# The head of a two-layer attention kernel: idle products, the place of the first projection, centred weights, maxima as a step

## The chip, the cores and the metric

The kernel runs on one core of a Trainium2 chip. The metric is the device time of one execution in microseconds (us), as the median of several runs. In the profile PE is TensorE, PEld its weight loads, DVE is VectorE, ACT is ScalarE, POOL is GpSimd, and SP is the engine that issues most DMAs.

## What is computed

Input x has 8 images of 128 channels and 48 x 48 positions (N = 2304). Layer 0 is a masked attention over positions, on the group-normed input joined to 32 rows of position embeddings. Layer 1 is a full attention of the tokens with themselves, then a normalized linear layer with a recurrence over tokens.

```python
# layer 0
x0 = concat([_gn(x), pe], axis=1)                # _gn: 32 groups of 4 channels
q = lrelu(Wq @ x0 + bq); k = lrelu(Wk @ x0 + bk); v = lrelu(Wv @ x0 + bv)
attn = q.T @ k / sqrt(128), masked to the lower triangle
x = x + softmax(attn) @ v
# layer 1
t = tokens(x)
t = t + softmax(n @ n.T) @ n                     # n = _ln_t(t)
Wx = _ln_t(t) @ W.T, normalized over all images and tokens
y[i] = sigmoid(Wx[i] + y[i-1] @ V.T)             # over the tokens, y[-1] = 0
t = t + y
```

## The kernel before

One image after another goes through `Causal` (layer 0) and `Full` (attention of layer 1); the recurrence over all images comes last. N is cut into six chunks of 384 columns (`NQ = 6`, `QC = 384`), and each chunk into three blocks of 128 (`QB = 3`). For each pair of a key block m and a query chunk j there is a score product s (one bank of the four of pool `ps_s`), an exponential on ACT into p, and three items later (`LAG = 3`) an output product o. In float32 a product of 384 columns is two instructions. In the masked part VectorE also adds up p into `acc`.

Ahead of its scores a chunk n needs its projection, `project(b, n)`: `normed` applies the group norm (L872), and three `part`s each make a product with the weights of q, k or v (L879, L882; also in banks of `ps_s`), add the chunk's position term `pb` (L884) and apply the leaky ReLU (L889). In the third part follow two reductions that give the largest |q| and |k| (L893), the load of the position term of chunk n + 2 (`load_positions`, L850), and the next projection. Two projections' xn can exist at a time, and four q.

The position terms are the same for every image. `positions(n, j)` makes them from 33 rows (32 embeddings and the bias, L837 and L840), ACT copies them out (L841), and they are stored in DRAM once per chunk (L843, on SP's queue). Those of chunks 0 and 1 also stay on chip for the first image; all others are loaded again, into two buffers. The steps for chunks 2 to 5 form a chain named `making`; loading chunk n first advances it to 3 (n - 1) steps.

The order of instructions on every engine is written out by hand. A planner, `Stream`, holds a modelled time `now` and the time at which each engine is free. Work that isn't part of the main stream of scores and outputs is a chain of steps, each with a cost on TensorE, further costs on other engines, and a due time. After every item of the stream, `tick` runs up to two steps that are due, in the order in which the chains were added. `advance` and `finish` run a chain's steps regardless of the due time. These planned times only fix the order in which instructions are issued; the engines wait for each other through semaphores.

At the start of the program x is loaded in three pieces on SP (L711), followed there by half of the position rows, w, V and gamma and beta (L741 to L744). TensorE runs 12 idle products of the identity with itself (L1383), then the position products of chunk 0. The group norm of image 0 is three parts: BN_STATS and BN_AGGR on VectorE (L796, L798), a product with `grp` that averages over a group (`gn_m`, L804), three small VectorE operations to `gn_e`, a second product (`gn_v`, L815), and a power on GpSimd (L665). Position products of chunk 1 lie between these. Then `project(0, 0)` is added, and the stream starts; its first item finishes that projection. `ffn_weights` (L746 to L756), due at a planned 30 us, centres w on VectorE, transposes it on TensorE, and makes V times one half; both products go into one bank.

The later projections are started in three places: chunks 1 and 2 at the end of the projection before them (`if n + 1 < EARLY`, with `EARLY = 3`), chunks 3 to 5 by row j = 0 to 2 of the stream (`begin`), and chunk 0 of the next image near the end of `Full`.

Of the kernel before, what the change touches and what calls it, by code (L numbers as in the profile page):

```python
# [16 lines left out]
ALU = mybir.AluOpType  # L17
AX = mybir.AxisListType
# [586 lines left out]
def fast_path(ctx: ExitStack, tc: tile.TileContext, x, pe, w_ffn, out, x_tok, w_qkv, w_pos, v_t, gamma_beta, flag):  # L605
# [61 lines left out]
    with ExitStack() as actx:  # L667
# [19 lines left out]
        def psum_t(name):  # L687
            return ps_t.tile([P, CH], F32, tag="t", name=name)
# [16 lines left out]

        xbuf = {}

        def load_x(b, pieces=2):
            xbuf[b] = big.tile([P, N], F32, tag="x", name=f"x_{b}")
            for h in range(pieces):  # L710
                nc.sync.dma_start(xbuf[b][:, ts(h, N // pieces)], x_v[b, :, ts(h, N // pieces)])  # L711

        load_x(0, 3)


        cg = C // GROUPS
# [26 lines left out]
        nc.sync.dma_start(vT_f, v_t)  # L743
        nc.sync.dma_start(gb, gamma_beta)  # L744

        def ffn_weights():  # L746

            s = small.tile([P, 1], F32, tag="gn_d", name="w_sum")
            nc.vector.tensor_reduce(s, w1, AX.X, ALU.add)
            nc.vector.tensor_scalar_mul(s, s, 1.0 / P)  # L750
            nc.vector.tensor_scalar(w1, w1, s, None, ALU.subtract)
            tp = psum_t("tp_ffn")
            nc.tensor.transpose(tp[:, 0:P], w1, ident)
            nc.vector.tensor_copy(w1T, tp[:, 0:P])
            nc.tensor.matmul(tp[:, P : P + 1], vT_f, half, start=True, stop=True)
            nc.vector.tensor_copy(v_half, tp[:, P : P + 1])  # L756


        same = apool.tile([P, R, SQ], F32, tag="same", name="same")
# [29 lines left out]
        def group_norm(b):  # L789
            xt = xbuf[b]  # L790
            c = {}

            def part1():
                gs = small2.tile([P, NQ, 6], F32, tag="gn_st", name=f"gn_st_{b}")
                for j in range(NQ):
                    nc.vector.bn_stats(gs[:, j, :], xt[:, ts(j, QC)])  # L796
                mv = small2.tile([P, 2], F32, tag="gn_mv", name=f"gn_mv_{b}")
                nc.vector.bn_aggr(mv, gs)  # L798
                c["mv"] = mv

            def part2():
                mv = c["mv"]
                tp = psum_t(f"gn_m_{b}")
                nc.tensor.matmul(tp[:, 0:1], grp, mv[:, 0:1], start=True, stop=True)  # L804
                mg = small2.tile([P, 1], F32, tag="gn_mg", name=f"gn_mg_{b}")
                nc.vector.tensor_copy(mg, tp[:, 0:1])
                d = small.tile([P, 1], F32, tag="gn_d", name=f"gn_d_{b}")
                nc.vector.tensor_sub(d, mv[:, 0:1], mg)
                e = small2.tile([P, 1], F32, tag="gn_e", name=f"gn_e_{b}")
                nc.vector.scalar_tensor_tensor(e, d, d, mv[:, 1:2], ALU.mult, ALU.add)  # L810
                c["mg"], c["e"] = mg, e

            def part3():
                tp = psum_t(f"gn_v_{b}")
                nc.tensor.matmul(tp[:, 0:1], grp, c["e"], start=True, stop=True)  # L815
                rs = small2.tile([P, 1], F32, tag="gn_rs", name=f"gn_rs_{b}")
                rsqrt(small2, rs, tp[:, 0:1], 1e-5, "gn")
                norm_of[b] = c["mg"], rs

            return [(part1, 0.0, [("DVE", 3.6)]), (part2, 0.15, [("DVE", 0.6)]), (part3, 0.15, [("DVE", 0.15), ("POOL", 0.9)])]  # L820
# [34 lines left out]
        def project(b, n):  # L855

            cols = ts(n, QC)
            c = {}

            def normed():  # L860
                if n > 1:
                    st.finish(projected[b, n - 2])
                if (b, n) in pos_loads:
                    st.finish(pos_loads[b, n])
                c["pb"] = pos.pop((b, n))
                if n == 0:
                    keys[b] = big.tile([P, N], F32, tag="k", name=f"k_{b}")
                    vals[b] = big.tile([P, N], F32, tag="vT", name=f"vT_{b}")
                    largest[b] = small2.tile([P, 2, NQ], F32, tag="largest", name=f"largest_{b}")
                mg, rs = norm_of[b]  # L870
                c["xn"] = chunk_tile("xn", f"xn_{b}_{n}", c, 4)
                nc.vector.tensor_scalar(c["xn"], xbuf[b][:, cols], mg, rs, ALU.subtract, ALU.mult)  # L872

            def part(j):
                def f():
                    xn = c["xn"]
                    ps = psum_s(f"pj_{b}_{n}_{j}")
                    if j < 2:
                        nc.tensor.matmul(ps[:, :QC], wT[:, j, :], xn, start=True, stop=True)  # L879
                    else:  # L880
                        for m in range(0, QC, P):
                            nc.tensor.matmul(ps[:, ds(m, P)], xn[:, ds(m, P)], wT[:, j, :], start=True, stop=True)  # L882
                    z = chunk_tile("z", f"z_{b}_{n}_{j}")
                    nc.vector.tensor_add(z, ps[:, :QC], c["pb"][:, j, :])  # L884
                    if j == 0:
                        queries[b, n] = qp.tile([P, QC], F32, tag="q", name=f"q_{b}_{n}")
                    dst = (queries[b, n], keys[b][:, cols], vals[b][:, cols])[j]

                    nc.vector.scalar_tensor_tensor(dst, z, 0.01, z, ALU.mult, ALU.max)  # L889
                    c[j] = dst  # L890
                    if j == 2:
                        for i in range(2):
                            nc.vector.tensor_reduce(  # L893
                                largest[b][:, i, n : n + 1], c[i], AX.X, ALU.max, apply_absolute_value=True
                            )
                        load_positions(*divmod(b * NQ + n + 2, NQ))
                        if n + 1 < EARLY:
                            project(b, n + 1)
                        if n == NQ - 1 and b + 1 < B:
                            st.add([(partial(load_x, b + 1), 0.0, [])], 5.0)  # L900

                return f

            steps = [(normed, 0.0, [("DVE", 0.75)])]

            steps += [(part(j), QC * US, [("DVE", 0.0 if j < 2 else 4.5)]) for j in range(3)]
            c["chain"] = projected[b, n] = st.add(steps)

        def bounds(b):
# [79 lines left out]
        class Causal:  # L989
# [18 lines left out]
            def begin(self, j, m, first):  # L1008
                b = self.b
                if first:  # L1010
                    st.finish(projected[b, j])
                    if j + EARLY < NQ:
                        project(b, j + EARLY)
                    if j == NQ - 1:
                        bounds(b)
                off = self.offset(j, m)
                s = psum_s(f"s_{b}_{j}_{m}")
                nc.tensor.matmul(s[:, off:QC], keys[b][:, ts(m, P)], queries[b, j][:, off:], start=True, stop=True)  # L1018
                p = pp.tile([P, QC], F32, tag="p", name=f"p_{b}_{j}_{m}")
                nc.scalar.activation(p[:, off:], s[:, off:QC], AF.Exp, scale=SCALE)  # L1020
                ops = [("ACT", 0.16 + (QC - off) * 0.00085)]
                if m >= QB * j:
                    nc.gpsimd.tensor_mul(p[:, off : off + P], p[:, off : off + P], triu)  # L1023
                    ops.append(("POOL", 0.5))
                return p, st.then(st.spend((QC - off) * US), ops)
# [350 lines left out]
                ], max(at, st.free["DVE"]) + 0.2 - st.now)  # L1376

        norm_chain = {}
        st.add([(ffn_weights, 0.3, [("DVE", 0.5)])], 30.0)
        def idle(tp, n):  # L1380

            for _ in range(n):
                nc.tensor.matmul(tp[:, :P], ident, ident, start=True, stop=True)  # L1383

        idle(psum_s("idle"), 12)
        for j in range(3):
            positions(0, j)
        gn = st.add(group_norm(0))
        st.advance(gn, 2)
        positions(1, 0)  # L1390
        st.finish(gn)
        for j in range(1, 3):
            positions(1, j)
        project(0, 0)
        making = st.add([(partial(positions, n, j), QC * US, [("ACT", 0.5)]) for n in range(2, NQ) for j in range(3)], 6.0)


# [13 lines left out]
        for n in range(len(stream) + LAG):  # L1411
            if n < len(stream):
                part, j, what, first, last = stream[n]
                ready[n] = part.begin(j, what, first)
            if n >= LAG:
                part, j, what, first, last = stream[n - LAG]
                if first:
                    o[part, j] = psum_o(f"o_{n}")
                part.product(j, what, o[part, j], *ready.pop(n - LAG), first, last)
                if last:  # L1420
                    part.after(j, o.pop((part, j)))
            st.tick()
# [194 lines left out]
```

## Time and profile before

| | us |
|---|---|
| median of three runs | 1761.54 (1758.81 to 1763.01) |
| profiled execution | 1763.07 |
| its span, first to last instruction | 1761.4 |
| PE busy in the span | 1733.7 |
| scores of `Full`, L1217: 1008 instructions | 409.3 |
| outputs of `Full`, L1231 and L1227: 1728 instructions | 683.8 |
| scores and outputs of `Causal`, L1018 and L1029: 2016 instructions | 761.2 |
| projections, L879: 192 instructions | 80.6 |
| wait of PE for w on VectorE, L753 | 1.5 |
| wait of PE for xn, L879 | 1.4 |
| wait of PE for the aggregated statistics, L804 | 1.4 |
| wait of VectorE for a position load, L884 | 4.4 |

The first four rows frame the run: the profiled execution lies 1.7 us above its own span. The product rows are busy times of TensorE; an instruction there overlaps the next one, so they add up to more than the span. The four waits are all in the first 36 us. "Granted clock" in the views below is the share of its full clock that TensorE was given.

### The profile page before, as it was taken

Reading aid. Unit: us, or ns where it says so; the run is one execution under the profiler, and the core shown is the slowest. Engines: PE = TensorE matmul, PEld = TensorE weight load, DVE = VectorE, ACT = ScalarE, POOL = GpSimd, SP = SyncE. Lnnn points to the kernel's source line nnn. Section 1 sums busy time; section 2 is a strip of 40 time slices with the busy share of each in tenths; the row PEclk is TensorE's granted clock in tenths of the full one; section 3 lists DMA queues with packets and bytes.
Section 4 is the critical chain, followed back from the end, with each engine's and each line's share of the span. In section 5 each row is a group of like instructions: output and inputs, shape, how many; then the busy total and the mean of one; then the engine's idle time right before and its main releaser. Section 6 shows DMA issues by size and latency. Waiting matters only on the chain.

```text
span 1761.4 us, 21442 instructions
## 1 busy us (share of the span) xinstructions
PE 1733.7 (98%) x6134; PEld 1082.0 (61%) x6135; DVE 1159.5 (66%) x3163; ACT 718.9 (41%) x1332; POOL 321.0 (18%) x397
## 2 busy tenths in 40 slices
PE   8999999999999999999999999999999999999986
PEld 5666666656666566666666566665666666665565
DVE  4875569655886459755696557864587556974357
ACT  2344334443344424443244433444344432444345
POOL 1131002300132001410024001320014100240006
PEclk7999999999999999999999999999999999999998
DMA  3415673157533684156731575335941568216768
GB/s 128 144 32 185 174 202 117 63 178 208 161 93 110 182 223 138 41 178 178 205 117 61 181 203 158 99 111 175 229 140 41 172 178 211 62 56 181 204 214 217
DMA packets 206050, 261.94 MB, mean 149 GB/s; under 512 B 90113, under 2 KB 175010, under 8 KB 205412
## 3 DMA queue, kind: packets, MB, share of 16 engines
q1 hardware_dynamic: 204972, 257.47, 50.3%
q0 software_dynamic: 720, 2.62, 1.0%
q8 instruction: 51, 0.84, 0.2%
q14 instruction: 75, 0.61, 0.1%
q10 hardware_dynamic: 232, 0.40, 0.1%
HBM read 150.24 MB, written 110.17 MB: 148 GB/s over the span
## 4 chain that ended last, share of the span: by engine, by line
PE 96%; DMA 1%; DVE 1%; SPq 1%; issue 0%; ACT 0%; POOL 0%; DVEq 0%; ACTq 0%; POOLq 0%
PE s L1217 18%; PE o L1231 18%; PE s L1018 17%; PE o L1029 17%; PE o L1227 13%; PE pj L879 4%; PE pj L882 2%; PE z L1530 2%; PE wx L1306 2%; PE tb L939 1%; PE of_t L939 1%; PE pb L837 0%; DMA x<-in_x_dram 0%; PE dn L1077 0%; DMA t2x<-t_d 0%; DMA out_dram<-r 0%
## 5 line engine op out<-in xcount | busy, mean ns | idle before, releaser
L1219 ACT ACTIVATE p<-s,shift 128x384 f32<-128x384 f32 x504 | 292.5, 580 | 519.0 <-PE s L1217 497.8
L1217 PE MATMUL s<-xh 128*128 128x384 f32 x1008 | 409.3, 488 | 0.0
L1020 ACT ACTIVATE p<-s 128x384 f32<-128x384 f32 (+2 forms) x504 | 231.0, 460 | 427.3 <-PE s L1018 349.3
L1231 PE MATMUL o<-p,xhT 128*128 128x384 f32 x1008 | 402.4, 486 | 1.1 <-ACT p L1219 1.1
L1018 PE MATMUL s<-q,k 128*128 128x384 f32 (+2 forms) x1008 | 382.9, 462 | 0.2 <-DVE k L889 0.2
L1029 PE MATMUL o<-p,vT 128*128 128x384 f32 (+2 forms) x1008 | 378.3, 457 | 0.0
L1227 PE MATMUL o<-g,xhT 128*128 128x384 f32 x720 | 281.4, 486 | 1.1 <-DMA g<-e 1.1
L1188 DVE STREAM_TRANSPOSE t<-p 128x384 f32<-128x384 f32 x360 | 186.1, 550 | 136.2 <-ACT p L1219 97.6
L1231 PEld LDWEIGHTS o<-p,xhT 128*128 128x128 f32 x1008 | 190.2, 190 | 129.2 <-ACT p L1219 1.7
L1217 PEld LDWEIGHTS s<-xh 128*128 128x128 f32 x1008 | 187.4, 190 | 119.5
L1029 PEld LDWEIGHTS o<-p,vT 128*128 128x128 f32 x1008 | 188.5, 191 | 116.1 <-POOL p L1023 3.0
L1018 PEld LDWEIGHTS s<-q,k 128*128 128x128 f32 x1008 | 182.3, 191 | 96.7 <-issue 1.3
L1044 DVE TENSOR_TENSOR acc<-acc,p 128x384 f32<-128x384 f32 (+2 forms) x408 | 213.4, 523 | 26.5 <-POOL p L1023 2.9
L1227 PEld LDWEIGHTS o<-g,xhT 128*128 128x128 f32 x720 | 134.1, 190 | 87.7 <-issue 1.8
L1023 POOL TENSOR_TENSOR p<-p,triu 128x128 f32<-128x128 f32 x144 | 77.8, 544 | 528.9 <-ACT p L1020 527.6
L884 DVE TENSOR_TENSOR z<-pj,pb 128x384 f32<-128x384 f32 x144 | 79.4, 551 | 137.5 <-PE pj L879 120.3
L1280 POOL TENSOR_TENSOR roots<-ve_f,mhalf 128x3 f32<-128x3 f32 x48 | 42.0, 876 | 500.7 <-DVE ve_f L923 500.7
L1114 POOL TENSOR_SCALAR xhT<-xhT 128x384 f32<-128x384 f32 x48 | 60.8, 1267 | 187.5 <-PE tb L939 187.5
L879 PE MATMUL pj<-xn,wT 128*128 128x384 f32 x192 | 80.6, 505 | 1.4 <-DVE xn L872 1.4
L1307 DVE TENSOR_TENSOR scale<-wx,scale 128x384 f32<-128x384 f32 x46 | 25.6, 556 | 69.2 <-PE wx L1306 59.9
L1258 DVE TENSOR_REDUCE dn<-of_t 128x3 f32<-128x384 f32 x48 | 26.6, 554 | 67.5 <-PE of_t L939 67.5
L1115 POOL TENSOR_SCALAR t1t<-t1t 128x384 f32<-128x384 f32 x48 | 61.3, 1277 | 0.0
(237 smaller groups left out, 1469.9 us busy)
## 6 DMA issues: line engine op xcount, KB each, us to landing
e<-t SPq DMA_DIRECT2D x120, 576.0 KB
g<-e SPq DMA_DIRECT2D x480, 144.0 KB
pb<-posb_d SPq DMA_DIRECT2D x46, 576.0 KB
t1t<-in_x_tok_dram SPq DMA_DIRECT2D x48, 192.0 KB
t_d<-tt SPq DMA_DIRECT2D x184, 48.0 KB
t2x<-t_d SPq DMA_DIRECT2D x46, 192.0 KB
scale<-rs SPq DMA_DIRECT2D x46, 192.0 KB
x<-in_x_dram SPq DMA_DIRECT2D x14, 576.0 KB
```

Source lines behind the costliest of these rows:

```text
L879: nc.tensor.matmul(ps[:, :QC], wT[:, j, :], xn, start=True, stop=True)
L884: nc.vector.tensor_add(z, ps[:, :QC], c["pb"][:, j, :])
L1018: nc.tensor.matmul(s[:, off:QC], keys[b][:, ts(m, P)], queries[b, j][:, off:], start=True, stop=True)
L1020: nc.scalar.activation(p[:, off:], s[:, off:QC], AF.Exp, scale=SCALE)
L1023: nc.gpsimd.tensor_mul(p[:, off : off + P], p[:, off : off + P], triu)
L1029: nc.tensor.matmul(o[:, off:QC], vals[b][:, ts(m, P)], p[:, off:], start=first, stop=last)
L1044: nc.vector.tensor_add(a[:, off:], a[:, off:], p[:, off:])
L1188: nc.vector.transpose(t[:, :, :, g, :].rearrange("p b j r -> p j b r"), p.rearrange("p (j b r) -> p j b r", j=QB, b=R))
L1217: nc.tensor.matmul(s[:, :QC], xh[:, ts(m, P)], xh[:, ts(j, QC)], start=True, stop=True)
L1219: nc.scalar.activation(p, s[:, :QC], AF.Exp, bias=shift)
L1227: nc.tensor.matmul(out_ap, xhT[:, QB * i + g, :], p, start=first, stop=last)
L1231: nc.tensor.matmul(o[:, :QC], xhT[:, what[1], :], p, start=first, stop=last)
```

## The change

The diff has six edits.

1. x of image 0 is loaded in pieces of 2, 2, 1 and 1 chunks, instead of three pieces of two chunks. Other images keep two pieces.
2. `ffn_weights` is split: `centre` does the three VectorE operations on w, and a planned 6 us later `ffn_weights` does the products, which now go into two banks.
3. The two reductions to the largest |q| and |k| leave the third part and become a step of their own, `measured`, the last of a projection. The planned cost is split accordingly (3.4 + 1.1 instead of 4.5).
4. Chunk 3's projection is started at the end of chunk 2's (`n < EARLY`) and no longer by row 0 (`if j and ...`); that holds for all images.
5. In the group norm of image 0, 14 idle products come ahead of `gn_m`, and 10 between `gn_m` and `gn_v`, where a position product of chunk 1 was. Two position products of chunk 1 follow the norm; then come the norm and three parts of chunk 0's projection and the norm of chunk 1, and only then the third position product.
6. After the third item of the whole stream's start (n = 2), `making` is advanced to one step, projection (0, 1) to four, and `making` to four.

```diff
-        def load_x(b, pieces=2):
+        def load_x(b, pieces=(3, 3)):
             xbuf[b] = big.tile([P, N], F32, tag="x", name=f"x_{b}")
-            for h in range(pieces):
-                nc.sync.dma_start(xbuf[b][:, ts(h, N // pieces)], x_v[b, :, ts(h, N // pieces)])
-
-        load_x(0, 3)
+            at = 0
+            for n in pieces:
+                nc.sync.dma_start(xbuf[b][:, ds(at, n * QC)], x_v[b, :, ds(at, n * QC)])
+                at += n * QC
+
+        load_x(0, (2, 2, 1, 1))
...
-        def ffn_weights():
+        def centre():
             s = small.tile([P, 1], F32, tag="gn_d", name="w_sum")
             nc.vector.tensor_reduce(s, w1, AX.X, ALU.add)
             nc.vector.tensor_scalar_mul(s, s, 1.0 / P)
             nc.vector.tensor_scalar(w1, w1, s, None, ALU.subtract)
-            tp = psum_t("tp_ffn")
+
+        def ffn_weights():
+
+            tp, tv = psum_t("tp_ffn"), psum_t("tp_half")
             nc.tensor.transpose(tp[:, 0:P], w1, ident)
+            nc.tensor.matmul(tv[:, 0:1], vT_f, half, start=True, stop=True)
             nc.vector.tensor_copy(w1T, tp[:, 0:P])
-            nc.tensor.matmul(tp[:, P : P + 1], vT_f, half, start=True, stop=True)
-            nc.vector.tensor_copy(v_half, tp[:, P : P + 1])
+            nc.vector.tensor_copy(v_half, tv[:, 0:1])
...
                     if j == 2:
-                        for i in range(2):
-                            nc.vector.tensor_reduce(
-                                largest[b][:, i, n : n + 1], c[i], AX.X, ALU.max, apply_absolute_value=True
-                            )
                         load_positions(*divmod(b * NQ + n + 2, NQ))
-                        if n + 1 < EARLY:
+                        if n < EARLY:
                             project(b, n + 1)
...
+            def measured():
+                for i in range(2):
+                    nc.vector.tensor_reduce(largest[b][:, i, n : n + 1], c[i], AX.X, ALU.max, apply_absolute_value=True)
+
-            steps += [(part(j), QC * US, [("DVE", 0.0 if j < 2 else 4.5)]) for j in range(3)]
+            steps += [(part(j), QC * US, [("DVE", 0.0 if j < 2 else 3.4)]) for j in range(3)]
+            steps += [(measured, 0.0, [("DVE", 1.1)])]
...
-                    if j + EARLY < NQ:
+                    if j and j + EARLY < NQ:
                         project(b, j + EARLY)
...
-        st.add([(ffn_weights, 0.3, [("DVE", 0.5)])], 30.0)
+        st.add([(centre, 0.0, [("DVE", 0.8), ("", 6.0)]), (ffn_weights, 0.3, [("DVE", 0.5)])], 30.0)
...
         gn = st.add(group_norm(0))
+        idle(psum_s("idle_m"), 14)
         st.advance(gn, 2)
-        positions(1, 0)
+        idle(psum_s("idle_e"), 10)
         st.finish(gn)
-        for j in range(1, 3):
+        for j in range(2):
             positions(1, j)
         project(0, 0)
+        st.advance(projected[0, 0], 4)
+        st.advance(projected[0, 1], 1)
+        positions(1, 2)
         making = st.add(...)
...
                 ready[n] = part.begin(j, what, first)
+                if n == QB - 1:
+                    st.advance(making, 1)
+                    st.advance(projected[0, 1], 4)
+                    st.advance(making, 4)
```

## The prediction

> **What bounds the kernel now.** I read the page's busy shares first, then its slices, then the stretches of the first 60 us, and last the timeline of the head.
>
> ```profile
> PE 1733.7 (98%) x6134; PEld 1082.0 (61%) x6135; DVE 1159.5 (66%) x3163; ACT 718.9 (41%) x1332; POOL 321.0 (18%) x397
> ...
> PEclk7999999999999999999999999999999999999998
> ```
>
> TensorE is the bound. Only the first and the last slice show it below full speed, so whatever the head saves arrives at the end, if the rest stays as it is. The stretches of the head (columns: time, busy time of PE, PEld, DVE, ACT, POOL, granted clock, DMA):
>
> ```profile
> 0.00:6.43 6.43, 4.77 (x24) 4.58 (x24) 1.02 (x2) 1.28 (x1) 5.04 (x28) 1.00 0.73 216
> 6.43:8.90 2.47, 2.19 (x10) 1.49 (x10) 1.43 (x3) 1.16 (x3) 0.00 (x0) 1.00 0.63 191
> 8.90:19.14 10.24, 9.13 (x23) 6.00 (x24) 3.93 (x12) 1.71 (x4) 0.57 (x1) 0.50 0.28 115
> 19.14:29.38 10.24, 8.51 (x39) 5.58 (x37) 7.94 (x18) 3.96 (x9) 1.57 (x3) 1.00 0.36 124
> 29.38:39.62 10.24, 9.85 (x17) 4.80 (x17) 3.08 (x8) 1.24 (x3) 0.00 (x0) 0.50 0.36 127
> 39.62:49.86 10.24, 10.17 (x42) 5.76 (x40) 6.32 (x15) 3.05 (x8) 0.91 (x2) 1.00 0.33 114
> 49.86:59.10 9.24, 7.86 (x34) 5.30 (x35) 7.60 (x17) 2.67 (x6) 0.45 (x1) 1.00 0.26 75
> ```
>
> PE looks busy, but in 8.9 to 19.1 and 29.4 to 39.6 at half the clock. I price what was done. The groups by shape in 0 to 59.1 count 47 products of 384 columns (positions 18, projections 15, scores 9, outputs 5; two instructions each, or six of 128), four of 256 and four of 128. At full clock one of 384 takes 0.645 (the chain of waits lists one per 0.65), so 30.3 + 1.7 + 0.9 + some 0.6 of small ones = 33.5 us. The head therefore loses 59.1 - 33.5 = 25.6: 6.4 before the first position product, 8.2 up to the end of score (0,2) at 27.9 (13.3 of work in 21.5), and 11 after it (20.2 in 31.2). Where the losses sit:
>
> ```profile
> 10.01 0.56 PE L804 MATMUL gn_m<-gn_mv,grp 128*128 128x1 f32 x2 [1.35 <-DVE gn_mv L798]
> ...
> 12.06 0.58 PE L815 MATMUL gn_v<-gn_e,grp 128*128 128x1 f32 x2
> ...
> 19.69 0.88 PE L1018 MATMUL s<-q,k 128*128 128x384 f32 x2 [0.24 <-DVE k L889]
> ...
> 29.38 0.47 PE L753 MATMUL tp_ffn<-ident,w 128*128 128x128 f32 x1 [1.50 <-DVE w L751]
> ...
> 35.45 0.56 DVE L884 TENSOR_TENSOR z<-pj,pb 128x384 f32<-128x384 f32 x1 [4.42 <-DMA pb<-posb_d]
> ```
>
> PE waits for the group mean, later for w behind VectorE's queue (1.50); the second wait is followed by 10.24 us at half clock. Then VectorE waits 4.42 for a position load: by the planner's times, worked through by hand, that is chunk 3, projected before chunk 2.
>
> **What the Trainium skill says.** "TensorE: Matmul & The Clock Gate", Part 1, section "What's actually happening": the clock is halved after an idle window of about 3.4 us, restored after a busy one, and the window runs free of the kernel. The trace agrees on the grid: changes at 8.90, 19.14, 29.38, 39.62, steps of 3 x 3.41. It does not agree that the window must be empty: PE was busy 2.19 of the 2.47 us ahead of 8.90. Those were products with 33 rows, so I estimate that a window counts by rows used. The same page, Part 2, "Step-by-step", says matmuls stay in program order: an idle product ahead of gn_m delays it. [...]here store to dependent load took 23.27 to 26.20 = 2.9, and load to use 31.45 to 35.45 = 4.0.
>
> **The change, part by part.**
>
> *Loading x in 2,2,1,1 chunks.* One issue more on SP (0.41), which moves the second half of the positions, w, V and gamma back by that; the first of them used is the half for chunk 3, after 20 us. After the last landing one BN_STATS is left instead of two (0.5 sooner; smaller pieces could give back as much). It doesn't count either way, since PE comes later to gn_m.
>
> *Idle products.* 14 and 10, two instructions each, at 0.107 (six of 128 columns per 0.645): 3.0 and 2.15 us. The first position products end at 8.66, so gn_m moves from 10.01 to 11.65. VectorE needs 1.2 from gn_m to gn_e; with 0.2 for gn_m and the ten products, gn_v starts at 14.0 (before 12.06). gn_v to xn took 1.48, xn 0.48: the first projection can start at 15.95, against 15.43. So some 2 us are paid, and the clock stays whole if rows count as I think: 8.9 to 12.3 is filled; the window 19.1 to 22.5 is the weakest, and one with the same mix stayed at 1.00 before.
>
> *First projection ahead of positions(1,2).* Positions (1,0), (1,1) take 1.3 beside the root and xn, so they are hidden. At full clock z starts 0.85 after its projection (23.19 to 24.04) and VectorE's six steps take 3.27 (24.04 to 27.3): z at 16.8, k ready at 19.0, v at 20.1, score (0,0) at 19.15 (before 19.69). Position (1,2) fills part of PE's wait. *Maxima as a step:* the two reductions (0.92) go behind the next xn, which ends at 20.5 instead of 22.0; projection 1 no longer waits for them. The work itself is unchanged.
>
> *PE's order by the planner's times:* s00, three positions of chunk 2, q1, s01, k1, a position, s02, v1, position, s10, o00, position, s11, o01, position, s12, o02, position, q2, s13, and so on. The new advances of `making` find their steps mostly done. Each change between 33-row and 128-row products costs 0.1 (21.90 to 22.66 for one of 0.645). Adding these up, PE ends score (1,0) at 27.0 and the last position product at 42.3. Against 59.1 before, it then lacks three scores and six projections of 384 columns, one output of 256 and one of 128: 9 x 0.645 + 0.43 + 0.21 = 6.45, so 48.75. That is 10.35 us sooner.
>
> *Centring sooner.* The three VectorE instructions (28.54 to 29.33) now run 6 planned us ahead of the transpose: 1.50 + 0.39 of PE's waits go, v_half goes to another bank. VectorE's 0.8 lies where it waits for projections anyway; without that cover it costs 0.8.
>
> *What is late next.* Chunk 4 is added when row 1 begins, chunk 3 only when 2 is projected. So chunk 4's position load is issued at about 43.3, behind store 5 on SP, and lands at 47.3, while its z could start at 44.4. VectorE stands some 3 us; behind z queue the sums acc, and PE hits the fourth score bank after about 3 us of other work. I take 1.2 for that and as much for chunk 5: 2.4 (ends 0, if the banks last, and 6, if the load also waits for store 5). VectorE was busy 58% of 20 to 57 us (22 of 37) and would be near 80%; enough, with little slack.
>
> *The seven later heads.* Chunk 3's projection follows chunk 2's, instead of waiting for row 0. No instruction more; its 5 us of VectorE move out of a full stretch:
>
> ```profile
> 235.00:245.00 10.00, 10.00 (x39) 6.32 (x39) 7.37 (x22) 1.45 (x3) 1.72 (x3) 1.00 0.96 238
> 245.00:255.00 10.00, 10.00 (x40) 6.50 (x39) 6.04 (x15) 4.75 (x8) 0.45 (x1) 1.00 0.59 191
> 255.00:265.00 10.00, 10.00 (x39) 6.48 (x38) 9.51 (x27) 3.00 (x7) 1.70 (x4) 1.00 0.32 101
> ```
>
> PE is full either way: 0, with ends of -1 and +14 (below).
>
> Sum: 10.35 - 2.4 = 8 us. Against the profiled execution, 1763.07 - 8 = 1755.1. That run lies 1.5 above the median of 1761.54; the free clock window may be why, and I take half of it: 1754.3.
>
> **Rivals.**
> 1. *The clock falls all the same*, in a window of mostly 33-row products. Observed drops lasted 10.24 us, which costs 5: 1759.5. For it: the drop at 8.90 came at a busy PE. Against: idle products fill the next window.
> 2. *VectorE becomes the bound* in the first rows (9.5 of 10 us busy in the second head): half of the gain returns, 1759. Against: its waits of 14.8 in 20 to 57 leave room.
> 3. *The reorder does less than it says.* If positions and projections fall as before and only the clock and the centring change, about 5 remain: 1758.
> 4. *Slower.* In each later head the third projection needs score banks while VectorE is behind with the last full row; PE then stands at its z. At 1.15 us per head, seven heads eat the 8; at 2 us it is +14 - 8 = 6 slower, 1769. For it: all banks are shared. Against: VectorE is at 60 to 74% there, and turned products need no such bank.
>
> **Numbers.** Main case (gain 5.5 to 11) 0.63; rival 1 0.12; 2 0.09; 3 0.07; 4 0.09. About 0.2%, 3.5 us, is what a measurement here can tell from nothing, so "faster" is below 1758.0: the main case, half of 3 and some of 1 and 2, 0.72. Rival 4 is slower, 0.09; same 0.19. Range: from the main case with no stall and two us of luck, 1750.5, to rivals 1 and 2, 1760.
>
> **What would show it.** Right: clock 1.00 from 5.5 on; gn_m near 11.7, gn_v near 14; score (0,0) near 19.2; no wait of tp_ffn for w; z of chunk 4 waiting 2 to 3 us for pb; PE full from about 50. Wrong: a stretch at 0.50 after 9 us, a PE wait at a projection in a later head, or a later row's start that isn't some 8 us earlier at 100 us as at 1600.

## The result, and the profile after

The changed kernel is slower: 1770.62 us (median of 6, 1765.71 to 1772.77) against 1759.93 (median of 6, 1758.35 to 1763.01); the ratio is 1.0056, interval 1.004 to 1.0071. The prediction was 1754.3, faster, with a range up to 1760. The profiled execution took 1769.84, its span 1768.0; before it was 1763.07 and 1761.4.

Where along the program does the difference arise? One product that each image has is a good milestone: `gn_m` of images 1 to 7, in us from the start, as the groups by tile give it.

```
                 img 1   img 2   img 3   img 4   img 5    img 6    img 7    span
before           154.0   359.9   565.7   771.6   977.5   1183.4   1389.3  1761.4
after            159.2   365.0   570.8   776.5   982.2   1188.8   1394.5  1768.0
```

The loss is complete at image 1 (+5.2) and the same at image 7 (+5.2); 1.4 more come at the end. Between these two milestones both kernels take 1235.3 us, so the seven later heads cost nothing in this pair of profiles. (The twelve profiles of this document take 1234.8 to 1237.7 us there with the fourth edit in the later images, and 1235.3 to 1237.2 without it.) So the head of image 0 is the place. The busy shares and the clock of the page hardly show it:

```profile
PE 1736.7 (98%) x6183; PEld 1086.9 (61%) x6183; DVE 1160.4 (66%) x3163; ACT 718.8 (41%) x1332; POOL 324.4 (18%) x397
...
PEclk9899999999999999999999999999999999999998
```

The first slice has a better clock than before, the second a worse one. The stretches of the changed kernel (columns as before: time, busy time of PE, PEld, DVE, ACT, POOL, granted clock, DMA):

```profile
8.90:19.14 10.24, 10.24 (x73) 8.62 (x72) 3.07 (x10) 1.90 (x4) 0.57 (x1) 1.00 0.15 59
19.14:29.38 10.24, 10.03 (x41) 5.75 (x41) 7.59 (x16) 4.41 (x10) 1.48 (x3) 1.00 0.43 160
29.38:39.62 10.24, 10.24 (x41) 6.20 (x41) 4.79 (x13) 3.56 (x8) 0.96 (x2) 1.00 0.52 189
39.62:49.86 10.24, 10.24 (x42) 6.03 (x42) 4.36 (x11) 3.57 (x8) 0.46 (x2) 1.00 0.36 106
49.86:59.10 9.24, 3.76 (x13) 2.50 (x12) 5.59 (x12) 0.38 (x1) 0.53 (x2) 0.80 0.37 119
59.10:80.00 20.90, 18.83 (x64) 11.96 (x63) 17.21 (x42) 4.37 (x10) 2.20 (x5) 0.84 0.43 150
```

Up to 50 us it goes as forecast: whole clock, PE full. Then PE is busy for 3.76 of 9.24 us, and the clock is halved from 55.4 to 62.2 and from 65.6 to 69.0. The timeline of that place, by engine:

```profile
45.90 0.42 DVE L1050 TENSOR_TENSOR acc<-acc,p 128x256 f32<-128x256 f32 x1
52.63 0.56 DVE L889 TENSOR_TENSOR z<-pj,pb 128x384 f32<-128x384 f32 x1 [6.31 <-DMA pb<-posb_d]
...
55.42 0.47 DVE L877 TENSOR_SCALAR xn<-x,gn_mg,gn_rs 128x384 f32<-128x384 f32 x1
...
49.73 0.83 PE L887 MATMUL pj<-wT,xn 128*128 128x128 f32 x6
56.04 1.62 PE L884 MATMUL pj<-xn,wT 128*128 128x384 f32 x2 [5.48 <-DVE xn L877]
...
37.80 8.23 SPq L848 DMA_DIRECT2D posb_d<-pb  x2
46.14 0.37 SPq L855 DMA_DIRECT2D pb<-posb_d  x1
46.55 0.90 SPq L972 DMA_DIRECT2D o_d_c<-ot_c  x1
```

VectorE reaches the z of chunk 4 at 46.3 and waits 6.31 for the position load, which was issued at 46.14, right after store 5 (the row at 37.80 joins stores 4 and 5; the second was issued at 45.71). Six instructions later on VectorE comes xn of chunk 3, and the next product in PE's order is the projection of chunk 3, which needs it: PE stands 5.48. A stretch of 3.41 us passes with PE empty (51.97 to 55.38), and the clock falls. Later PE stands once more, at the projection of chunk 5:

```profile
65.25 0.30 PEld L884 LDWEIGHTS pj<-xn,wT 128*128 128x128 f32 x2 [2.65 <-issue]
65.28 1.29 PE L884 MATMUL pj<-xn,wT 128*128 128x384 f32 x2 [2.07 <-DVE xn L877]
```

This second wait is of another kind. The load of chunk 5 was issued at 56.39, and the z of chunk 5 starts at 66.61 without a wait. But from 57.7 to 64.7 VectorE works through eleven instructions with one wait of 0.72, and xn of chunk 5 is behind them. The last two of the eleven are maxima, which the third edit was to put behind the next xn.

The other waits that the prediction named went as it said: there is none of `tp_ffn` for w, nor of `gn_m` for the statistics. TensorE's waits for xn, before and after (waited for: total, times, longest):

```profile
PE pj L879 <- DVE xn L872: 1.4, 1, 1.4
...
PE pj L884 <- DVE xn L877: 7.5, 2, 5.5
```

### The profile page after: what moved, and what is told of

Read it like the earlier page. It is cut to its first block, busy times and chain, and to the rows that moved or that the text cites. A ratio compares the mean times of both kernels' runs of the same rounds, so it can differ in the third digit from the quotient of the medians.

```text
span 1768.0 us, 21483 instructions
## 1 busy us (share of the span) xinstructions
PE 1736.7 (98%) x6183; PEld 1086.9 (61%) x6183; DVE 1160.4 (66%) x3163; ACT 718.8 (41%) x1332; POOL 324.4 (18%) x397
## 4 chain that ended last, share of the span: by engine, by line
PE 97%; DMA 1%; DVE 1%; issue 0%; ACT 0%; SPq 0%; POOL 0%; DVEq 0%; POOLq 0%; ACTq 0%
PE s L1223 18%; PE o L1237 18%; PE s L1024 17%; PE o L1035 17%; PE o L1233 13%; PE pj L884 4%; PE pj L887 2%; PE wx L1312 2%; PE z L1544 2%; PE of_t L945 1%; PE tb L945 1%; PE pb L842 1%; DMA g<-e 0%; DMA pb<-posb_d 0%; PE dn L1083 0%; PE idle L1389 0%
## 5 line engine op out<-in xcount | busy, mean ns | idle before, releaser
L1050 DVE TENSOR_TENSOR acc<-acc,p 128x384 f32<-128x384 f32 (+2 forms) x408 | 209.8, 514 | 25.4 <-DVE acc L1050 0.5
L935 POOL TENSOR_TENSOR rs_c<-ve_c,mhalf 128x3 f32<-128x3 f32 x48 | 50.4, 1051 | 82.7 <-DVE ve_c L929 81.4
L1313 DVE TENSOR_TENSOR scale<-wx,scale 128x384 f32<-128x384 f32 x46 | 25.6, 556 | 57.6 <-PE wx L1312 49.7
```

What stands on the lines that cost most here:

```text
L1050: nc.vector.tensor_add(a[:, off:], a[:, off:], p[:, off:])
```

## The experiments

Theory A was formed on this trace: a projection that comes ahead of the one before it waits for a position load that was issued only just before, and holds up VectorE and then TensorE. Theory B blamed the fourth edit as such, others the idle products or the fuller VectorE. All ratios are to the kernel before, on the same chip.

### Edit 4 undone, or alone

```diff
-                        if n < EARLY:
+                        if n + 1 < EARLY:
...
-                    if j and j + EARLY < NQ:
+                    if j + EARLY < NQ:
```

Expected: 

> The change with its fourth edit undone (chunk 3 started by row 0 again, chunk 4 by row 1). Theory A, a projection issued ahead of the one before it waits for a position load that was issued only just before, and VectorE holds up the rest: then the order is 0, 1, 3, 2 again, the wait moves from chunk 4 to chunk 3 (VectorE 4 to 6 us for pb, TensorE standing and some 7 to 10 us at half clock after it), and the time stays above the kernel before, 1762 to 1771 against its 1760. Theory B, the fourth edit by itself is what costs and the other five bring the forecast 8: 1750 to 1755.

Measured: 1759.62 (20 runs) against 1760.61, ratio 0.9998 (0.9988 to 1.0009), which is in neither range. Two of the 20 runs took 1770.4 and 1770.6, at a lower mean clock (0.990 and 0.989; the others 0.995 to 0.996). The expected wait moved to chunk 3, but its price didn't come with it:

```profile
34.83 0.91 PE L884 MATMUL pj<-xn,wT 128*128 128x384 f32 x2
...
35.49 0.56 DVE L889 TENSOR_TENSOR z<-pj,pb 128x384 f32<-128x384 f32 x1 [5.50 <-DMA pb<-posb_d]
35.58 0.81 PE L1024 MATMUL s<-q,k 128*128 128x384 f32 x2
```

VectorE waits 5.50, nearly as long as in the change, and PE no time at all: what lies in its order there are scores and outputs of row 1, positions, and products with an xn that is ready. `gn_m` of image 1 comes at 145.9, against 159.2 in the change and 154.0 before. So my expectation was half wrong: the wait alone does nothing; it costs where PE's next product needs something that VectorE has behind it.

The same edit put alone on the kernel before. Expected: 

> The kernel before with the fourth edit alone. Theory A: chunk 4 now comes ahead of 3 in place of 3 ahead of 2; the wait for the load of chunk 3 goes, one for that of chunk 4 comes, 3 to 7 us, so that the two nearly cancel: 1757 to 1766. Theory B, the fourth edit costs by itself, in this head or in the later ones: 1768 or more.

Measured: 1766.18 (6 runs), ratio 1.0035 (1.0022 to 1.0047). That is just above theory A's upper end of 1766 and below B's 1768. The chain is the same: VectorE waits 5.2 for the load, PE 6.8 in two waits for xn, and `gn_m` of image 7 lies 3.2 behind the first profile, that of image 1 1.2; against the second profile of the kernel before, shown below, image 1 is 6.2 behind. The edit costs some 6 us there and 10 to 12 within the change.

### All chunks in order

```diff
-                        if n < EARLY:
+                        if n < EARLY or (b == 0 and n + 1 < NQ):
...
-                    if j and j + EARLY < NQ:
+                    if b and j and j + EARLY < NQ:
```

Expected: 

> The change with chunks 4 and 5 of image 0 started at the end of the chunk before them, so that all six come in order; later images as in the change. Theory A: VectorE waits under 1 us for any position load, no half clock after 5.5 us, first rows dense; 6 to 11 us below the kernel before, 1749 to 1754. Rival, the idle products and the compressed VectorE work are what costs: TensorE then waits elsewhere, 1760 or more.

Measured: 1758.77 (13 runs, 1755.79 to 1774.63), ratio 0.9995 (0.9984 to 1.0006): 12 us below the change, but no faster than the kernel before, so neither the gain of theory A came nor the waits elsewhere of its rival. No wait of VectorE for a position load in the head is left, and none of PE for xn. VectorE has the same work here as in the change, so a fuller VectorE alone does not make PE wait; the order of the projections has to come to it. The profiled execution, however, was the slowest of the 13, and shows something else. The windows of 3.41 us around the fall (the second answer is for the 33-row products of lines 842 and 845 alone, PE and PEld):

```profile
14.91:18.33 3.42, 3.42 (x16) 2.06 (x15) 1.83 (x4) 0.96 (x2) 0.41 (x1) 1.00 0.02 5
18.33:21.74 3.41, 3.20 (x15) 1.93 (x15) 3.13 (x7) 1.55 (x4) 0.45 (x1) 1.00 0.41 170
21.74:25.15 3.41, 3.41 (x10) 2.40 (x10) 0.85 (x2) 0.89 (x3) 0.00 (x0) 0.50 0.35 146
49.05:52.46 3.41, 3.41 (x7) 2.08 (x7) 1.56 (x3) 0.86 (x2) 0.22 (x1) 0.50 0.42 173
```

```profile
18.33:21.74 3.41, 1.55 (x4) 0.67 (x4) 1.00 0.41 170
...
18.33:21.74 3.41, 0.97 (x9) 0.96 (x9) 1.00 0.41 170
```

PE was busy for 3.20 of 3.41 us and the clock fell all the same; 2.52 of the 3.20 were position products with 33 rows. It then stayed at half for nine windows, until 52.46, with PE full throughout. This is rival 1 of the prediction. If each busy time is weighted by rows, 33/128 for positions and 1 for the rest, the windows of five profiles sort, with one exception ("no idle" and "edit 4" are the change without its idle products, shown below, and the kernel before with edit 4 alone):

```
window          profile    busy  positions  share by rows  clock after it
 5.48 to  8.89  before     3.12    2.35        0.40        falls
19.13 to 22.54  before     3.17    2.19        0.45        stays
25.96 to 29.37  before     1.93    1.67        0.20        falls
18.33 to 21.74  in order   3.20    2.52        0.39        falls
 4.67 to  8.09  in order   3.05    1.86        0.49        stays
18.47 to 21.88  no idle    3.41    2.74        0.40        falls
66.26 to 69.67  no idle    1.41    0.00        0.41        falls
62.84 to 66.26  no idle    1.49    0.00        0.44        stays
21.25 to 24.66  change     3.41    2.13        0.54        stays
21.74 to 25.15  in order   3.41    0.91        0.80        stays at half
55.38 to 58.79  change     2.75    0.00        0.81        stays at half
54.43 to 57.85  edit 4     2.82    0.00        0.83        rises
29.37 to 32.78  before     3.01    0.00        0.88        stays at half
49.05 to 52.46  in order   3.41    0.20        0.96        rises
```

By busy time alone they don't sort: 3.41 and 3.20 fell, 1.49 and 3.05 stayed. The exception is the window of 0.88, which held a transpose and products of one column, whose busy time says little. The borders aren't sharp: the positions are two lines whose busy times overlap a little. By my estimate from the same traces, with each moment counted once, the falls at 0.39 to 0.40 come to about 0.43 to 0.44.

A second profile of the same kernel. Expected: 

> The version with all chunks in order once more, for a second profile. Theory: the window that fell at 21.7 us in the first one lies elsewhere, no fall after 5.5 us, the group-norm product of image 1 at 143 to 148 (161.2 there, 154.0 before), total 1755 to 1760. Rival: a fall at the same place again.

Measured: 1760.4, `gn_m` of image 1 at 148.2. There was a fall at 21.79 again, so the rival's words came true, but it lasted one window (to 25.20) and not nine. The windows of the two executions happened to lie 0.05 us apart (4.67 and 4.72), so this pair doesn't show whether the place of a fall moves; the two profiles of the kernel before do. Total and milestone are just above the ranges of the theory.

### Without the idle products

```diff
-        idle(psum_s("idle_m"), 14)
...
-        idle(psum_s("idle_e"), 10)
```

Expected: 

> The change without its 24 idle products in the group norm. Theory A: the wait of VectorE for the load of chunk 4 stays, 5 to 7 us, with the half clock behind it; gn_m comes 3 us sooner, but the clock falls at about 9 us as before and the first projection runs at half speed; 1765 to 1773, within 4 us of the change. Rival, the idle products are what makes it slower: 1762 or less.

Measured: 1768.53 (6 runs), ratio 1.0042 (1.0027 to 1.0056). The wait for the load stays (4.8), and the clock falls at 11.64, 21.88, 69.67 and 76.50. These come from the slowest of the six runs, 1785.08, whose second fall lasted 30.7 us; the median is what counts. The interval overlaps that of the change, so the idle products aren't what makes it slower.

### The load of chunk 4 ahead of store 5

```diff
                         load_positions(*divmod(b * NQ + n + 2, NQ))
+                        if b == 0 and n == 2:
+                            st.finish(pos_loads[0, 4])
```

Expected: 

> The change, with the position load of chunk 4 issued as soon as the last part of chunk 2 has been issued, ahead of store 5 on SP; the order of projections stays as in the change (4 ahead of 3). Theory A: the load is issued at 43.7 in place of 46.1 and lands in 4 to 5 us since no store runs beside it, so VectorE's wait of 6.3 goes down to 0.5 to 3, TensorE's of 5.5 to 0 to 1.5, without a fall of the clock there; 1758 to 1765. Rival, the wait is made by the order of the projections and not by the load: 1768 to 1771.

Measured: 1762.86 (11 runs), ratio 1.0019 (1.001 to 1.0028); 7 to 8 us of the change's loss are gone by one DMA issued earlier, and the waits lie in the ranges of theory A. SP's queue, VectorE and PE:

```profile
43.28 0.32 SPq L855 DMA_DIRECT2D pb<-posb_d  x1
45.36 0.32 SPq L848 DMA_DIRECT2D posb_d<-pb  x1
...
47.30 0.56 DVE L889 TENSOR_TENSOR z<-pj,pb 128x384 f32<-128x384 f32 x1 [1.34 <-DMA pb<-posb_d]
...
50.90 0.88 PE L884 MATMUL pj<-xn,wT 128*128 128x384 f32 x2 [0.70 <-DVE xn L877]
...
51.83 0.56 DVE L889 TENSOR_TENSOR z<-pj,pb 128x384 f32<-128x384 f32 x1
...
57.10 0.54 DVE L911 TENSOR_REDUCE largest<-k 128x1 f32<-128x384 f32 x1
57.56 0.47 DVE L877 TENSOR_SCALAR xn<-x,gn_mg,gn_rs 128x384 f32<-128x384 f32 x1
...
58.09 1.65 PE L884 MATMUL pj<-xn,wT 128*128 128x384 f32 x2 [3.04 <-DVE xn L877]
```

Issued 2.9 us sooner, the load took 4.0 (43.28 to 47.30) instead of 6.5 (46.14 to 52.63): store 5 now follows it by 2.1 us, where it went 0.4 ahead. That the two share the DMA engines is the likely reason; no run varies it alone, and with the same neighbours the load took 5.3 in the version with edit 4 alone. VectorE waits 1.34, PE 0.70. The second wait, of chunk 5, has grown to 3.04, and a window at half clock follows it. No load is waited for there: VectorE runs from 51.83 to the xn at 57.56 without a wait. So the rest of the loss is VectorE's, in the order that edit 4 makes, and theory A doesn't cover it: 0.70 + 3.04 and an estimated 1.7 for the clock (half of 3.41) are 5.4 of the 6.0 us by which image 1 (151.9) is behind the version with edit 4 undone. No run changed VectorE's queue at this place, so that part is read from the trace alone.

### The kernel before once more

Expected: 

> The kernel before once more, for a second profile of its head. Theory A': the clock window runs free of the program, so the places of the two falls (8.9 and 29.4 us) and their cost change from one execution to the next; the first profile, 1763.07 against a median of 1760.6, had the dear kind. Then the falls lie elsewhere here, and the group-norm product of image 1 comes 1 to 5 us ahead of the 154.0 of the first profile. Rival, the head is fixed and the spread comes from the later images: falls within 0.2 us of the same places, product at 154.

Measured: 1759.91. The falls lie at 11.29 and 28.36 and last 6.8 and 3.4 us, where the first profile had 8.89 and 29.38 with 10.2 each:

```profile
8.90:19.14 10.24, 9.85 (x28) 6.24 (x29) 5.43 (x14) 1.93 (x4) 0.57 (x1) 0.67 0.28 115
19.14:29.38 10.24, 8.36 (x38) 5.83 (x37) 6.23 (x16) 3.47 (x8) 1.57 (x3) 0.95 0.48 174
29.38:39.62 10.24, 10.24 (x35) 5.42 (x33) 5.53 (x13) 3.28 (x7) 0.00 (x0) 0.88 0.25 78
```

`gn_m` of image 1 comes at 149.0, 5 us ahead of the first profile. So the places and the length of the falls change from one execution to the next, and the head that the prediction started from was a dear one.

### Positions with all 128 rows

If rows count, position products with 95 rows of zeros keep the clock, at the same number of columns.

```diff
+        nc.vector.memset(wpT, 0.0)
+        for h in range(2):
+            nc.vector.memset(pe_sb[h], 0.0)
...
-            pe_c = pe_sb[n // (NQ // 2)][: NPE + 1, ts(n % (NQ // 2), QC)]
+            pe_c = pe_sb[n // (NQ // 2)][:, ts(n % (NQ // 2), QC)]
...
-                nc.tensor.matmul(ps[:, :QC], wpT[: NPE + 1, j, :], pe_c, start=True, stop=True)
+                nc.tensor.matmul(ps[:, :QC], wpT[:, j, :], pe_c, start=True, stop=True)
```

(The products of the third part lose `[: NPE + 1]` likewise.) On the version in order. Expected: 

> The version with all chunks in order, with the position products padded from 33 to 128 rows by zeros (three memsets on VectorE ahead of their loads); same columns, same results. Theory: the window counts busy rows, so a stretch of mostly 33-row products is taken for idle; with 128 rows no window falls, no execution of 1764 to 1775 is left (3 of 13 without the padding), 1751 to 1759. Rival, rows don't matter (or zeros count as idle), and the clock falls by other reasons: again about a quarter of the executions above 1763.

Measured: 1755.56 (11 runs, 1753.33 to 1757.48), ratio 0.997 (0.9961 to 0.9979). No execution lies above 1758, and the profile has no fall in the head:

```profile
8.90:19.14 10.24, 10.17 (x72) 8.53 (x71) 1.83 (x8) 2.39 (x5) 0.57 (x1) 1.00 0.15 59
19.14:29.38 10.24, 9.78 (x49) 6.80 (x49) 8.38 (x17) 4.32 (x10) 1.74 (x3) 1.00 0.41 147
29.38:39.62 10.24, 10.18 (x44) 6.73 (x44) 5.87 (x16) 3.80 (x9) 0.97 (x2) 1.00 0.60 218
```

The same without the 24 idle products. Expected: 

> The version in order with padded position products, without the 24 idle products. Theory: the idle products put gn_m and gn_v some 3 us later than they need to be and are of use only as filling; without them the first score comes 1 to 3 us sooner, but TensorE has two real waits between 9 and 14 us, so that a window that lies on both counts under 0.4 and falls in some executions: median 1752 to 1757, spread wider than the 4 us with them. Rival, the idle products still hold the clock in every execution: 1758 or more without them.

Measured: 1752.95 (4 runs, 1751.76 to 1754.96), ratio 0.9954 (0.9937 to 0.9971). `gn_m` of image 1 comes at 140.7, against 145.1 with the idle products. The falls that I expected in some executions don't show: none in the head of the profile, and the runs spread by 3 us. This is the fastest version, 7.4 us below the kernel before. With only four runs, whose upper end overlaps the lower end of those with idle products (1753.33), I take it as shown that the idle products aren't needed there, and only as likely that they cost time.

The padding alone on the kernel before. Expected: 

> The kernel before with padded position products alone. Theory: the fall at 8.9 to 11.6 us goes in most executions, the one at 28 to 29 stays where TensorE waits for w and half a window is empty; 1 to 4 us faster, 1756 to 1760. Rival, the gain of the padded version is all due to the order of projections: no difference, 1760 to 1762.

Measured: 1754.64 (6 runs), ratio 0.9968 (0.9956 to 0.9981). The early fall is gone; the one at 26.1 to 29.6, where PE waits 2.0 for w, stays for one window. That is more than the 1756 to 1760 I had expected: the padding alone on the kernel before brings more than the change's other five edits together (0.9998).

## Why the prediction was wrong

**Idle products and first projection: right, 1 us late.** `gn_m` came at 12.68 (forecast 11.65), `gn_v` at 15.14 (14.0), score (0,0) at 20.15 (19.15). The first position product already began at 7.05, not 6.46, and this part of the shift goes through all three. It is chance: the idle products at the start, which the change leaves alone, took 5.49 us here, and 4.77 and 4.28 in the two profiles of the kernel before. The whole clock up to 50 us was as forecast.

**Centring, PE's order, later heads: right.** The waits for w are gone, the order worked out from the planner's times has 4 ahead of 3 as in the trace, and the later heads cost 0. The maxima went behind the next xn at first (21.46, 28.63), but later also ahead of it (44.12, 63.75).

**The sum up to the last position product: 2.8 us too good.** That product ends at 45.1 (forecast: 42.3). What remains to be done from there is what the prediction counted: in the trace, too, the change lacks three scores, six projections and one output of 384 columns against the kernel before at 59.1. So it was 7.6 ahead at this point, not 10.35. The first score was 1.0 late; the other 1.8 came between 20 and 45 us, where PE was busy nearly throughout.

**What is late next: the step that failed.** Place and mechanism were named, z of chunk 4 at a load behind store 5; the term was 2.4 us for both chunks, and 6 at worst. It measured 5.48 + 2.07 of waits, and 10.2 us at half clock, an estimated 5.1 more: 12.7. The milestones agree: 7.6 ahead at the last position product and 5.2 behind at image 1 make 12.8. With that the sum changes sign; the version with row 0's start of chunk 3 has none of it and reaches image 1 at 145.9, 13.3 ahead of the change. Four things were off. The load was issued at 46.1 instead of 43.3 and took 6.5 instead of 4.0, beside store 5; I had noted the neighbour, but only for the worst case. PE did not run to the fourth score bank: the next projection's xn stands behind the waiting z on VectorE, and PE meets it first. I had priced a wait of PE without the clock that it takes away, though the profile before showed just this after the wait for w. And for chunk 5 the cause was wrong: no load was late, VectorE's queue was.

**The base: a second error of 5 us.** The losses of 25.6 were those of one execution with two falls of 10 us. The second profile of the same kernel has half of that, and its head is 5 shorter. I took off half of the 1.5 us by which the profiled run stood above the median; that was no measure of what the head varies by. So even without the stall the change is worth nothing that could be told: 0.9998 and 0.9995 in the two versions without it. In the profile with edit 4 undone, image 1 is 8.1 ahead of the first profile of the kernel before, but 3.1 ahead of the second, and by the end of the span 1.1 are left of these; 2.5 us of waits for loads of `g` lie in the images between, against 0.2 in that second profile.

**The rivals.** Rival 1 (the clock falls all the same) is real, in the version in order: 3 of 13 executions took 1764 or more, and the one of them that was profiled shows it. Rival 2 (VectorE becomes the bound) came true in one place, the second wait. Rival 3 (the reorder does less than it says) holds in part: 7.6 of the 10.35. The slower rival was put in the later heads, where nothing happened. Its mechanism, PE standing at a projection whose VectorE is held up, is close to the right one, in the wrong place: I had it in hand for seven heads, and for the first one gave it 1.2 us. Small slips in the prediction's sums change nothing: rivals 2 to 4 are counted from 1763.07, without the 0.8 that the main case takes off, and by its own terms the lower end of the range is 1749.9, not 1750.5.

The 1.4 us that the change loses after image 7 are not peculiar to it. In its profile the clock is halved from 1700.6 to 1704.0, near the end of the program, and in the first profile of the kernel before it is not. The second profile of the kernel before has such a fall too, from 1680.4 to 1683.8, and takes 373.5 us from image 7 to the end, as the change does; the first took 372.1.

## What to carry to other kernels

When work is brought forward, follow every instruction queued behind its first wait on the same engine, and ask which of them the busiest engine needs next: a VectorE wait of 5.5 us cost nothing in one order of TensorE, and one of 6.3 was the greater part of 12.7 in another. Price a TensorE wait with the halved clock that can follow it. And where a profile shows clock falls, take a second profile of the same kernel before counting them as gain: the falls in the two profiles of the kernel before lasted 3.4, 6.8 and 10.2 us, and one in the version in order 30.7.

## What the hardware showed that I had not expected

The Trainium skill, "TensorE: Matmul & The Clock Gate", Part 1, section "What's actually happening", has the clock halved after an idle window. Here it also fell after windows with PE busy for 3.1 to 3.4 of 3.41 us, when most of it were 33-row products; the measurement decides. By the count of the table, windows up to a share by rows of 0.41 fell and those from 0.44 kept the clock; it rose again at 0.83 and at 0.90 or more, and not at 0.81, nor in the one of 0.88. These are readings of a few windows, not exact limits. Zeros fill the rows as well as data (no fall in the head of both padded versions in order), which speaks for the rows in use, whatever their values.

Products of 33 rows between those of 128 also cost a gap: in the change the last position product of chunk 2 starts at 22.39 and the projection after it at 23.14, 0.75 for 0.645 of work; with padded rows it is 22.78 to 23.45, 0.67.

A load of 576 KB that was waited for took 4.0 to 4.2 us from issue to use in four profiles in which no store was issued within 2 us of it, and 6.5 and 5.3 in two profiles with a store of the same size issued 0.4 us ahead of it.
